# Later requests for masks and residuals, earlier rows for the next group, and a reordered last gate in a graph layer kernel

## The chip, the cores and the metric

The kernel runs on one core of one Trainium2 chip. The metric is the device time of one execution in microseconds (us). Of several executions the median is given; one further execution was profiled, and every number on instructions, waits and transfers comes from that one.

## The reference

The input is a batch of 32 graphs of 512 nodes with 256 features, and a 512 x 512 mask `adj` for each. All numbers are 32-bit floats. The layer is, for each graph:

```
h      = relu(layernorm(x))
c1     = relu(bn1(conv1d_1tap(h)))                 # 256 -> 256 channels
x_conv = relu(bn2(conv1d_17taps(c1)) + h)          # along the 512 nodes
s      = h @ w_se.T + b_se                         # 3 numbers a node
A      = exp(-|s_n - s_m|^2) * adj                 # 512 x 512
x_nmp  = A @ relu(h @ w_msg.T + b_msg)
gi     = concat(x_conv, x_nmp) @ w_ih.T + b_ih     # 512 -> 768
gh     = h @ w_hh.T + b_hh                         # 256 -> 768
r, z   = sigmoid of the first two thirds of gi + gh
new    = tanh(gi_n + r * gh_n)
out    = x + (1 - z) * new + z * h
```

So there are three large blocks of matrix work: the 17-tap convolution, the masked product of the graph, and the gates r, z and new.

## The kernel before

**Layout.** A graph's features stand with channels on partitions (`hT`, two halves of 128 channels by 512 nodes). The 17-tap convolution is computed with a fast algorithm: the nodes of all graphs are cut into units of 18, the units are collected in seven groups (`STARTS`), and each group takes 25 products of transformed inputs (`x2`, `xd`) with transformed weights (`w`). In the first group the weights are made on the chip and stored to DRAM (`wd`); from the second group on they are read back through a ring of three buffers. In the second group VectorE also forms a third of each weight by an addition (`third_weight`).

**Streams.** The program is not written out by hand. Five Python generators, called streams, give out work: `rows` (one-tap convolution of the graphs of a group, `conv1`, which fills the group's input `h1`), `begins` (normalise and transpose a graph), `graphs` (messages, exponentials, mask, masked product), `conv` (the 25 products of each group) and `gates`. A loop at the end of the kernel function keeps a modelled time `now` for TensorE and modelled free times for VectorE and ScalarE (`dve.free`, `act.free`). A stream yields the modelled time at which it may go on, or a condition. Of the streams that may go on, the loop takes the one whose clock is furthest behind its share. `fill()` then lets VectorE run ahead of `now` by up to 1.5 us of modelled work. What comes out is one fixed order of instructions for each engine[...]. `later(t, f)` puts an action off to modelled time t, and `settle()` runs everything that was put off, at once.

**Queues.** Nearly all loads are issued by SyncE (SP) in one order: masks (`Graphs.ask`, a ring of four), residuals (`load_res`, a ring of two), weights, rows (`load_row`, in the ring of two `hT` buffers that the transposed graphs also use), and the inputs of the gates. A load into a buffer that is still in use waits at the head of the SP queue. Stores are issued by GpSimd (POOL).

**Lines that matter here.** `masked` (L887) multiplies one quarter of the exponentials by the mask and asks for the next mask at once. `update` (L1129), run with each z gate, asks for the other residual: `load_res(b + o, 1 - o)`. `all_rows` (L1259) starts a group's rows when `at_product >= 25 * g - 1`, that is, when the last product of the group before is taken up. In `gates`, after the z products, the stream runs `reset_hidden` (VectorE: (r + 1) times the hidden product) and yields `dve.free + 0.1` before the products of the new gate. For the very last half gate (the last graph, o = 1) the hidden product is cut in two parts (384 and 128 nodes), which are multiplied after the z gate; `mix_ahead` (L1080) is four VectorE instructions that prepare the output before the tanh.

**A product of groups 2 to 7.** Eight matmul records with `x2` (called x products below) go to one bank of `ps_c`; ScalarE copies the bank to its neighbour; sixteen records with `xd` (xd products) then add to both banks; ScalarE takes the result away. The exponentials of a graph (L877) use the same `ps_c` buffer for one of their four matmuls. Each float32 matmul of the program is two records in the profile.

## Time and profile before

| what | value |
|---|---|
| median of 3 executions | 2123.65 us (2122.25 to 2126.0) |
| the profiled execution, its own time | 2125.44 us |
| its span | 2123.3 us |
| TensorE busy | 2062.8 us, 97% of the span |
| VectorE busy | 1375.5 us, 65% |
| ScalarE busy | 815.2 us, 38% |
| GpSimd busy | 337.7 us, 16% |
| granted TensorE clock, mean | 0.989 |
| transfers | 383.07 MB, 180 GB/s on average |

PE is TensorE's matmuls, PEld its weight loads, DVE VectorE, ACT ScalarE, POOL GpSimd, SP SyncE. L126 and L135 are helper lines through which nearly all instructions are recorded, so groups are told apart by the tiles that they write and read. A row of the waits reads: engine, what it was about to do, what ended its idle time, then us in total, number of waits and the longest. A row of the timeline reads: start, duration, engine, line, operation, tiles, shapes, count, and in brackets the idle time before it with its releaser. A row of a table by stage gives the stretch, its length, the busy time of PE, PEld, DVE, ACT and POOL (with counts), the granted clock, the busy share of the DMA engines and GB/s.

### The profile page before, as it was taken

What the parts mean: (1) busy time and instruction counts of PE and PEld (TensorE: products, weight loads), DVE (VectorE), ACT (ScalarE), POOL (GpSimd) and SP (SyncE); (2) the same over time, 40 slices, a digit from 0 to 9 for tenths busy, and PEclk for the clock granted to TensorE, in tenths of its full rate; (3) what the DMA queues carried; (4) which work ended last, traced back from release to release, by engine and by line L of the source; (5) the groups of instructions that cost most, each with busy time, mean ns of one, the idle gap of its engine ahead of it and who ended that gap; (6) DMA issues with size and microseconds to landing.
All of it is one profiled execution on the core that took longest, in us unless ns stands there. A gap on an engine that the chain in (4) does not pass through costs nothing.

```text
span 2123.3 us, 25913 instructions
## 1 busy us (share of the span) xinstructions
PE 2062.8 (97%) x8768; PEld 1265.0 (60%) x8768; DVE 1375.5 (65%) x2448; ACT 815.2 (38%) x1431; POOL 337.7 (16%) x582
## 2 busy tenths in 40 slices
PE   9999799999999989999999999999999999999998
PEld 6888366655666646666556665456665566654443
DVE  6888477884768737786576765576875757653223
ACT  5544533334532335422454233544324532234121
POOL 2101121111201102111121111121111210112111
PEclk9999999999999999999999999999999999999999
DMA  7455887776776676676767777677676756525332
GB/s 280 165 184 180 273 231 197 196 180 206 210 198 173 209 171 183 187 214 174 201 190 204 189 186 202 181 181 216 191 187 180 190 163 175 150 64 139 86 92 40
DMA packets 546436, 383.07 MB, mean 180 GB/s; under 512 B 456576, under 2 KB 473472, under 8 KB 545664
## 3 DMA queue, kind: packets, MB, share of 16 engines
q1 hardware_dynamic: 512992, 282.17, 50.5%
q0 software_dynamic: 28624, 86.01, 12.9%
q10 hardware_dynamic: 4688, 13.24, 1.6%
q8 instruction: 70, 1.15, 0.2%
q14 instruction: 62, 0.51, 0.1%
HBM read 281.95 MB, written 99.35 MB: 180 GB/s over the span
## 4 chain that ended last, share of the span: by engine, by line
PE 93%; ACT 2%; DMA 2%; DVE 1%; issue 1%; SPq 0%; POOL 0%; ACTq 0%; DVEq 0%
PE ps_acc L135 46%; PE ps_c L135 24%; PE ps_g L135 20%; DMA hT<-hd 2%; PE ps_g L140 2%; PE ps_c L877 1%; ACT at L126 0%; PE ps_acc L145 0%; DMA w<-wd 0%; ACT z L126 0%; PE ps_acc L877 0%; DMA vec<-in_vecs_dram 0%; ACT n L126 0%; ACT part L126 0%; PE ps_g L877 0%
## 5 line engine op out<-in xcount | busy, mean ns | idle before, releaser
L135 PE MATMUL ps_acc<-xconv,wih 128*128 128x512 f32 (+1 forms) x772 | 363.9, 594 | 3.5 <-DVE ps_acc L126 2.1
L135 PE MATMUL ps_acc<-xnb,wih 128*128 128x512 f32 (+1 forms) x772 | 362.3, 593 | 0.0
L135 PE MATMUL ps_acc<-hTb,whh 128*128 128x512 f32 (+1 forms) x772 | 357.3, 592 | 0.0
L135 PEld LDWEIGHTS ps_c<-xd,w 128*128 128x128 f32 x2400 | 300.2, 191 | 70.4 <-issue 56.3
L135 PE MATMUL ps_c<-xd,w 128*128 128x135 f32 (+1 forms) x2400 | 304.8, 280 | 4.8 <-ACT ps_c L126 4.8
L135 PEld LDWEIGHTS ps_c<-x,w 128*128 128x128 f32 x2000 | 253.5, 192 | 88.7 <-issue 54.7
L135 PE MATMUL ps_c<-x,w 128*128 128x135 f32 (+2 forms) x2000 | 262.4, 280 | 17.5 <-ACT z L126 6.3
L1093 POOL DMA_DIRECT2D out_dram<-res x252 | 164.0, 657 | 640.0 <-DVE res L126 580.4
L135 PEld LDWEIGHTS ps_acc<-xconv,wih 128*128 128x128 f32 x772 | 140.9, 191 | 147.5 <-issue 141.3
L135 PE MATMUL ps_g<-at,msg 128*128 128x512 f32 x512 | 227.4, 592 | 0.5 <-DVE at L126 0.5
L135 PEld LDWEIGHTS ps_acc<-hTb,whh 128*128 128x128 f32 x772 | 140.6, 190 | 144.8 <-issue 142.5
L135 PEld LDWEIGHTS ps_acc<-xnb,wih 128*128 128x128 f32 x772 | 141.0, 191 | 140.4 <-issue 138.4
L126 DVE TENSOR_TENSOR o_sb<-hTb,r 128x512 f32<-128x512 f32 x63 | 43.5, 690 | 211.3 <-ACT r L126 211.3
L135 PEld LDWEIGHTS ps_g<-at,msg 128*128 128x128 f32 x512 | 95.2, 190 | 110.5 <-issue 106.4
L126 DVE TENSOR_TENSOR msg<-ps_g,bmsg 128x256 f32<-128x256 f32 x128 | 53.8, 421 | 148.3 <-PE ps_g L135 148.2
L126 DVE SCALAR_TENSOR_TENSOR x<-x,x 128x544 f32<-128x544 f32 (+5 forms) x161 | 137.9, 856 | 3.3
L126 ACT ACTIVATE ps_c<-ps_c 128x270 f32<-128x270 f32 (+1 forms) x150 | 57.6, 384 | 206.1 <-PE ps_c L135 206.1
L135 PE MATMUL ps_g<-hT,w 128*128 128x512 f32 (+4 forms) x288 | 121.3, 570 | 14.7 <-DMA hT<-hd 14.7
L126 DVE TENSOR_TENSOR xd<-x 128x544 f32<-128x544 f32 (+1 forms) x150 | 107.4, 719 | 37.4 <-PE ps_c L135 37.2
L126 DVE TENSOR_TENSOR x<-x 128x272 f32<-128x272 f32 (+5 forms) x280 | 127.0, 499 | 0.3
L135 PE MATMUL ps_g<-wmsg,hTg 128*128 128x259 f32 x496 | 121.3, 381 | 0.0
L126 ACT ACTIVATE h<-ps_g,bn_shift,bn_scale 128x252 f32<-128x252 f32 (+4 forms) x208 | 85.8, 487 | 84.8 <-PE ps_g L135 84.7
(124 smaller groups left out, 2278.3 us busy)
## 6 DMA issues: line engine op xcount, KB each, us to landing
w<-wd SPq DMA_DIRECT2D x125, 768.0 KB, 5.2
m_sb<-in_adj_dram SPq DMA_DIRECT2D x384, 64.0 KB, 3.4
hd<-hT POOLq DMA_DIRECT2D x32, 512.0 KB, 6.0
hT<-hd SPq DMA_DIRECT2D x32, 512.0 KB, 4.6
hTb<-hd SPq DMA_DIRECT2D x32, 512.0 KB, 5.1
xnb<-nd SPq DMA_DIRECT2D x64, 256.0 KB, 3.3
xconv<-cd SPq DMA_DIRECT2D x32, 512.0 KB, 5.4
res<-in_x_dram SPq DMA_DIRECT2D x256, 64.0 KB, 3.8
```

The lines of the kernel that those rows point to most:

```text
L126: getattr(self.engine, name)(*tiles, **more)
L135: nc.tensor.matmul(ps, lhsT, rhs, **more)
L140: nc.tensor.transpose(ps, a, ident)
L877: nc.tensor.matmul(pss[c], gr.left[k, :], gr.right[k, :], start=True, stop=True, tile_position=(32 * c, 0),)
L1093: queue.dma_start(OB[b][:, s.start // 32 : s.stop // 32, o * P + 32 * g : o * P + 32 * g + 32], y[at, s].rearrange("i (k j) -> i k j", j=32),)
```

## The change

It has five parts.

1. In `masked`, from the ninth graph on, the next mask is asked for 1.5 us of modelled time after the mask's transpose, instead of right after the multiplication; a mask that was not asked for by then is asked for when it is needed.
2. A residual's buffer is asked for 5 us of modelled time after the store that empties it, instead of with the z gate; `mix_last` and `mix_ahead` ask for it if that has not happened.
3. The products of the new gate wait for `hidden_at`, the modelled end of `reset_hidden` plus 0.3 us, instead of `dve.free + 0.1`.
4. A group's rows may start when product `25 * g - 4` is taken up instead of `25 * g - 1`.
5. For the last half gate, the hidden product in two parts is computed before the z gate, and the `settle()` and the wait ahead of the remaining products go.

```diff
     def masked(b, at, c):
+        if (b, c) not in gr.masks:
+            gr.ask(NT * b + c + 1 - gr.asked)
...
         dve.transpose(gr.right, gr.masks.pop((b, c)))
+        later(dve.free + 1.5, lambda: gr.ask(1))
         dve.tensor_tensor(at[:, c, :], gr.right, at[:, c, :], op=ALU.mult)
-        gr.ask(1)
...
         def mix_last(r, z, o, s):
+            load_res(b, o)
             y = XR[b, o]
...
         def mix_ahead(z, o):
+            load_res(b, o)
             y = XR[b, o]
...
             if s.stop == N:
                 del XR[b, o]
+                later(now + 5.0, lambda: load_res(b + 1, o))
...
-                if b == o == 0:
+                if b == 0:
                     load_res(b, o)
...
+            hidden_at = 0.0
             def reset_hidden():
+                nonlocal hidden_at
                 while halves:
...
+                    hidden_at = dve.free + 0.3
...
             def update():
                 nonlocal z
-                load_res(b + o, 1 - o)
...
             if ps_h is not None:
                 reset_later(ps_h)
+            else:
+                parts = []
+                for s in (slice(0, N - P), slice(N - P, N)):
+                    ps = acc.tile([P, N], F32, name="ps_acc")
+                    parts.append((ps, s))
+                    for i in range(ND):
+                        matmul(
+                            ps[:, s], whh[:, i, cols(o, 2)], hT[:, i, s],
+                            start=(i == 0), stop=(i == ND - 1), skip_group_check=True,
+                        )
+                    hidden_half(ps, s)
+                    reset_later(ps, s)
+                    yield now
             ps_z = acc.tile([P, N], F32, name="ps_acc")
...
                 reset_hidden()
-                yield dve.free + 0.1
+                yield hidden_at
...
             later(act.free + 0.2, lambda: mix_ahead(z, o))
-            parts = []
-            for s in (slice(0, N - P), slice(N - P, N)):
...
-                yield now
-            settle()
-            yield dve.free + 0.1
             for ps, s in parts:
...
-                    freed >= g - 1 and begun > b and not turning and at_product >= 25 * g - 1
+                    freed >= g - 1 and begun > b and not turning and at_product >= 25 * g - 4
```

More of the change, by code (lines that the diff above doesn't have):

```diff
@@ L1178, in gates @@
             later(act.free + 0.2, lambda: mix_ahead(z, o))
-            parts = []
-            for s in (slice(0, N - P), slice(N - P, N)):
-                ps = acc.tile([P, N], F32, name="ps_acc")
-                parts.append((ps, s))
-                for i in range(ND):
-                    matmul(
-                        ps[:, s], whh[:, i, cols(o, 2)], hT[:, i, s],
-                        start=(i == 0), stop=(i == ND - 1), skip_group_check=True,
-                    )
-                hidden_half(ps, s)
-                reset_later(ps, s)
-                yield now
-            settle()
-            yield dve.free + 0.1
             for ps, s in parts:
```

## The prediction

> **What bounds the kernel now.** I read the page first: busy times and the chain that ended last.

> ```profile
> PE 2062.8 (97%) x8768; PEld 1265.0 (60%) x8768; DVE 1375.5 (65%) x2448; ACT 815.2 (38%) x1431; POOL 337.7 (16%) x582
> ...
> PE 93%; ACT 2%; DMA 2%; DVE 1%; issue 1%; SPq 0%; POOL 0%; ACTq 0%; DVEq 0%
> ```

> TensorE sets the end: 93% of the chain is matmuls, and no other engine is above 65%. So a change that leaves the matmuls alone can gain only what TensorE loses between them. Next, what TensorE waited for:

> ```profile
> PE ps_g L135 <- DMA hT<-hd: 14.7, 4, 7.9
> PE ps_c L135 <- ACT z L126: 6.6, 4, 4.8
> PE ps_c L135 <- ACT at L126: 6.0, 9, 0.7
> PE ps_c L135 <- ACT n L126: 5.1, 6, 1.3
> PE ps_c L135 <- ACT ps_c L126: 4.8, 9, 0.5
> ...
> PE ps_acc L135 <- DVE ps_acc L126: 2.1, 1, 2.1
> ```

> The first row is the loads of a new group's rows. The others are products placed right behind what they depend on, and the tail. Ends of matmuls are modelled, so I also took the distance of consecutive matmul starts less what such a matmul takes in a dense stretch (429 ns for 512 columns, some 113 ns for 135): TensorE loses about 78 us in all that way. The table by stage and the timeline show the largest place, where the second group begins:

> ```profile
> 210.42 0.49 SPq L830 DMA_DIRECT2D whh<-in_w_hh_dram  x1
> 210.96 0.94 SPq L831 DMA_DIRECT2D wih<-in_w_ih_dram  x1
> ...
> 215.22 0.40 SPq L210 DMA_DIRECT2D hT<-hd  x1
> ```

> ```profile
> 221.00:230.00 9.00, 1.05 (x3) 0.29 (x2) 2.55 (x3) 1.66 (x5) 1.08 (x2) 0.71 1.01 396
> 230.00:235.00 5.00, 5.00 (x7) 1.90 (x7) 0.69 (x1) 1.27 (x3) 0.54 (x1) 0.50 1.13 299
> 235.00:240.00 5.00, 5.00 (x15) 2.52 (x14) 0.00 (x0) 1.75 (x4) 0.00 (x0) 0.99 0.73 180
> ```

> The row load of 215.22 stands behind 2.25 MB of gate weights and takes 14.4 us in the chain; TensorE idles until 229.7 and then runs at half clock (0.50) for 5 us more. The same happens at 764 to 778. Last, an uncovered product and the tail:

> ```profile
> 1234.34 1.08 PE L135 MATMUL ps_c<-x,w 128*128 128x135 f32 x8
> 1235.95 1.30 PE L135 MATMUL ps_c<-xd,w 128*128 128x135 f32 x9 [0.53 <-ACT ps_c L126]
> ```

> ```profile
> 2111.80 0.69 DVE L126 SCALAR_TENSOR_TENSOR res<-part,res 128x512 f32<-128x512 f32 x1
> 2112.41 0.76 DVE L126 SCALAR_TENSOR_TENSOR ps_acc<-r,ps_acc 128x384 f32<-128x384 f32 x2
> 2113.02 1.56 PE L135 MATMUL ps_acc<-xconv,wih 128*128 128x384 f32 x4 [2.10 <-DVE ps_acc L126]
> ```

> Eight x records issue in 0.91 us; the xd product starts 1.61 us after their start: 0.70 us lost to ScalarE's copy. In the tail VectorE does `mix_ahead` first and TensorE's last products wait behind it.

> [...] SP stands 193.2 us in 51 waits for stores before residual loads, and 163.2 us in 51 before masks. [...]

> **The change part by part.** No work goes: the built programs have the same instructions on every engine, but for 4 warm-up transposes fewer (0.11 us each, put in where TensorE has nothing else). What moves is order, and I compared the two built orders.

> *Rows earlier.* Each batch's 512 KB load (issued in 0.3 to 0.4 us, landing in 4.6 at the median), its `conv1` matmuls, their six ACT evacuations (1.27 us for three) and the POOL memsets (about 0.5 us a boundary, 203.8 to 204.2) move some three products up. On SP all five loads of the second group now stand ahead of the 2.25 MB of gate weights. For every load I took the matmul work standing between what releases it and its first use: before, the shortest was 4.3 us, the load that stalled 5.9 us at 772; now the shortest is 8.9 us, the next 10.5, against 4.6 us of landing. So the 14.7 us go, hidden by products and gates; without that cover each load would cost up to 4.6 us. Half clock lasted about 5.3 us from 229.7 and 5.2 us from 772.8 (0.52), at half speed a loss of 2.65 and 2.5: 5.2 us go too. Moved ahead of stores on POOL, 0.5 us meets an engine 84% idle. Gate weights come later, but first use is some 17 us of matmuls off, against 12.7 us for the longer to land.

> *`hidden_at`.* `dve.free` is up to 1.5 us ahead of `now`, so the gates often could not go on and the scheduler put an xd product directly behind its x product. In the built order such pairs fall from 9 to 0, and an x product directly behind the last xd product from 7 to 0. From starts: 9 x 0.69 = 6.2 us, and 6 x 0.93 = 5.6 us (the seventh is the 4.8 us wait at 474, a late weight, left as it is). An exponential directly behind its transposes falls from 2 to 1: 1.4 us. Products directly behind the exponentials rise from 9 to 11: 2 x 0.82 = 1.6 us lost. If `hidden_at` is too early, the new gate waits for VectorE; the instruction takes 0.70 us and 0.3 is added, and matmuls whose feeder is under 1 us of matmul work back fall from 30 to 9. From nothing to 2 us; I take nothing.

> *Masks and residuals.* They cost TensorE nothing now: masks are used 29 us of matmuls or more after they are asked for, residuals 15 or more, and they land in 3.4 and 3.8. After: 24 and 18. Their price is what queues behind them on SP: weights, rows, gate inputs. Later masks leave SP freer. But residuals come nearer to their stores (median 3.5 us of matmuls between, before 6.4), since `settle()` often runs the delayed request at once. Before, the waits were 193.2/51 = 3.8 us each; I bound the change by -2 to +3 us for a request, hidden behind the covers above. What is late next is weights of group 2: loads with under 11 us of matmul work ahead of VectorE's addition rise from 10 to 13 (shortest 4.5; before 3.4). One of the ten cost 4.96 us and 1.7 us of half clock. I add 1.

> *Last gate.* VectorE's two parts now stand ahead of `mix_ahead`, which runs beside 3.5 us of matmuls: 2.1 us.

> Sum: -14.7 -5.2 -6.2 -5.6 -1.4 +1.6 -2.1 +1 = -32.6 us. The span becomes 2123.3 - 32.6 = 2090.7. The profiled execution took 2125.4, 1.8 over the median; against the median it is 2123.65 - 32.6 = 2091 us.

> **The rivals.** *Stalls come back elsewhere* (0.20). A scheduler's estimates miss anew in a new order. For it: VectorE stood 46.1 us in 20 waits for transposed input, with 14.7 in one, and the weights above. Two more stalls of 4.96 + 1.7 and a row load late by 4 give +17: about 2108. Against it: the fewer thin covers.

> *Residuals block SP, and it is slower* (0.08). The place is the row and weight loads queued behind a residual waiting for its store. Rows have about 13 us of cover less 4.6, so blocking decides from 8 us on; the longest now is 15.4. Above that each late load costs its delay and the clock, some 6.6 us as at 474. It takes five or more such (33/6.6), and with seven it is 2137. Only four residual requests fall among group 2's thin weight loads, which speaks against it.

> *Nothing comes of it* (0.04): row loads stall wherever they stand and the idle time moves: 2120 to 2127. Against it: the load at 215 was late because of what was ahead of it.

> *More comes of it* (0.06): the weight's stall (6.7) and the remaining half-clock stretches (about 8.5) vanish too: 2091 - 15 = 2076.

> **How the numbers follow.** The likeliest case (0.62) is 2091, its own range 2081 to 2101. 2078 to 2113 holds it, most of the second case and part of the last. About 0.2%, 4 us, is what a measurement of this kernel can tell from no change. Faster: 0.62 + 0.20 + 0.06 = 0.88; same 0.04; slower 0.08.

> **What would show it.** TensorE's wait for `hT<-hd` near zero and clock 1.00 around 215 to 240 and 765 to 780; nine waits for ACT `ps_c` gone; no DVE `ps_acc` wait in the tail; waits for `at` about 7 us. Wrong it would be with new TensorE waits behind late weights near 235 to 470 us, or with SP waiting for stores well over 193 us and rows late behind it.

## The result, and the profile after

The changed kernel takes 2117.15 us (median of 11, 2109.4 to 2122.01) against 2125.33 us for the kernel before (median of 11, 2122.25 to 2130.3): a ratio of 0.996, with a 95% interval of 0.9945 to 0.9974. It is faster by 8 us. 33 were forecast, and 2117 lies outside the range given. The profiled execution of the changed kernel took 2120.44 us, 3 us above the median, with a span of 2118.6.

The page, first its busy times, then the chain that ended last:

```profile
PE 2063.9 (97%) x8764; PEld 1263.2 (60%) x8764; DVE 1369.5 (65%) x2448; ACT 815.5 (38%) x1431; POOL 340.4 (16%) x582
...
PE 80%; issue 10%; DVE 3%; DMA 3%; ACT 2%; POOL 1%; SPq 1%; POOLq 0%; DVEq 0%; ACTq 0%
```

TensorE still sets the end. Four records fewer, the warm-up transposes, are all that is gone from it. Its waits in the changed kernel:

```profile
PE ps_g L135 <- DMA hT<-hd: 11.8, 6, 6.9
PE ps_acc L135 <- ACT xconv L126: 6.8, 1, 6.8
PE ps_c L135 <- ACT at L126: 6.7, 10, 0.7
PE ps_c L135 <- ACT ps_c L126: 3.5, 3, 1.9
PE ps_c L135 <- DVE x L126: 3.5, 1, 3.5
PE ps_g L140 <- DVE augl L126: 3.3, 1, 3.3
```

The wait for row loads, which was to go, is 11.8 us where it was 14.7. Nine waits for ScalarE's copy in `ps_c` have become three, but the three take 3.5 us where the nine took 4.8. The wait for `xconv`, an input of the gates, is 6.8 us where it was 1.4. Two waits for VectorE are new: 3.5 us for `x`, the transformed input of the convolution, and 3.3 us for `augl`, an input of the exponentials. The waits of the SP queue in the changed kernel show what has grown:

```profile
SPq L919 <- DMA out_dram<-res: 471.5, 104, 27.4
...
SPq L338 <- DVE right L126: 39.5, 16, 9.5
```

Before, SP stood 193.2 us in 51 waits for a store ahead of a residual load; now 471.5 us in 104. One request is four loads into a buffer that four stores empty, so SP can wait more than once for one request. Grouped by request, 23 of the 64 requests waited before, 8.4 us each, and 14 of them over 8 us; in the changed kernel 53 wait, 8.9 us each, and 27 of them over 8 us. The waits ahead of masks went the other way, from 163.2 to 39.5 us. The tail did as forecast. TensorE and VectorE in the timeline of the changed kernel:

```profile
2106.70 1.88 PE L135 MATMUL ps_acc<-xnb,wih 128*128 128x512 f32 x4
2108.42 1.45 PE L135 MATMUL ps_acc<-xconv,wih 128*128 128x384 f32 x4
```

```profile
2103.67 0.76 DVE L126 SCALAR_TENSOR_TENSOR ps_acc<-r,ps_acc 128x384 f32<-128x384 f32 x2 [2.75 <-ACT ps_acc L126]
2109.34 0.69 DVE L126 SCALAR_TENSOR_TENSOR part<-z,hTb 128x512 f32<-128x512 f32 x1 [4.91 <-ACT z L126]
```

VectorE's part (2103.67) now precedes `mix_ahead` (2109.34), and the last products follow without a gap: the 2.1 us are gone.

**How a residual request stalls TensorE.** The largest stall after is 6.9 us near 1380. From the timeline of the changed kernel, SP, then POOL, then TensorE:

```profile
1344.35 7.22 SPq L338 DMA_DIRECT2D m_sb<-in_adj_dram  x11
1356.66 1.97 SPq L919 DMA_DIRECT2D res<-in_x_dram  x4
...
1361.05 4.72 SPq L919 DMA_DIRECT2D x_sb<-xd  x8
...
1375.84 0.32 SPq L210 DMA_DIRECT2D hT<-hd  x1
```

```profile
1352.14 2.62 POOL L1097 DMA_DIRECT2D out_dram<-res  x4 [5.06 <-DVE right L126]
...
1370.21 0.54 POOL L954 DMA_DIRECT2D hd<-hT  x1 [6.13 <-DVE hT L126]
```

```profile
1382.05 2.62 PE L135 MATMUL ps_g<-hT,w 128*128 128x171 f32 x8 [6.88 <-DMA hT<-hd]
```

Read from the top: SP is done with its masks at 1351.6 and then stands for 4.9 us, because the next entry is a residual load whose buffer is being stored; POOL issues that store only at 1352.1. So the transposed input of the next graph (`x_sb<-xd`), behind the residual and four mask loads, leaves at 1361.1. VectorE's transposes wait for it, the store `hd<-hT` waits for VectorE (6.13 us), the row load waits for that store, since both use the two `hT` buffers, and TensorE waits 6.88 us for the row. The clock granted for the next 5 us is 0.50.

The other stall of that length, 6.8 us for `xconv` until 1712.1, looks different on SP:

```profile
1690.20 9.33 SPq L338 DMA_DIRECT2D m_sb<-in_adj_dram  x16
1701.12 2.11 SPq L919 DMA_DIRECT2D res<-in_x_dram  x4
1703.34 0.44 SPq L230 DMA_DIRECT2D xconv<-cd  x1
```

Issuing sixteen mask loads takes SP 9.33 us; in the same stretch it waits only 1.4 us for stores. The load of `xconv` stands mainly behind masks here. What the mask part has to do with it shows below.

### The profile page after: what moved, and what is told of

It reads as the page before. It is cut to its first block, busy times and chain, and to the rows that moved or that the text cites. A ratio compares the mean times of both kernels' runs of the same rounds, so it can differ in the third digit from the quotient of the medians.

```text
span 2118.6 us, 25907 instructions
## 1 busy us (share of the span) xinstructions
PE 2063.9 (97%) x8764; PEld 1263.2 (60%) x8764; DVE 1369.5 (65%) x2448; ACT 815.5 (38%) x1431; POOL 340.4 (16%) x582
## 4 chain that ended last, share of the span: by engine, by line
PE 80%; issue 10%; DVE 3%; DMA 3%; ACT 2%; POOL 1%; SPq 1%; POOLq 0%; DVEq 0%; ACTq 0%
PE ps_acc L135 40%; PE ps_c L135 21%; PE ps_g L135 17%; PE ps_g L140 1%; PE ps_c L877 1%; POOL out_dram L1097 1%; DMA hT<-hd 1%; DMA w<-wd 0%; DVE x L126 0%; PE ps_acc L145 0%; ACT at L126 0%; SPq L338 0%; PE ps_g L877 0%; DMA x_sb<-in_x_dram 0%; DMA xconv<-cd 0%
## 5 line engine op out<-in xcount | busy, mean ns | idle before, releaser
L135 PE MATMUL ps_acc<-xconv,wih 128*128 128x512 f32 (+1 forms) x772 | 365.2, 596 | 6.8 <-ACT xconv L126 6.8
L135 PE MATMUL ps_acc<-xnb,wih 128*128 128x512 f32 (+1 forms) x772 | 362.3, 594 | 0.0
L135 PE MATMUL ps_acc<-hTb,whh 128*128 128x512 f32 (+1 forms) x772 | 355.6, 590 | 0.0
L135 PEld LDWEIGHTS ps_c<-xd,w 128*128 128x128 f32 x2400 | 299.3, 190 | 73.2 <-issue 61.6
L135 PEld LDWEIGHTS ps_c<-x,w 128*128 128x128 f32 x2000 | 252.6, 191 | 90.7 <-issue 63.6
L135 PE MATMUL ps_c<-xd,w 128*128 128x135 f32 (+1 forms) x2400 | 302.2, 279 | 3.6 <-ACT ps_c L126 3.5
L135 PE MATMUL ps_c<-x,w 128*128 128x135 f32 (+2 forms) x2000 | 259.9, 278 | 13.8 <-ACT at L126 6.7
L135 PEld LDWEIGHTS ps_acc<-xconv,wih 128*128 128x128 f32 x772 | 141.6, 191 | 150.9 <-issue 140.9
L135 PE MATMUL ps_g<-at,msg 128*128 128x512 f32 x512 | 227.8, 596 | 0.6 <-DVE at L126 0.5
L135 PEld LDWEIGHTS ps_acc<-xnb,wih 128*128 128x128 f32 x772 | 141.2, 191 | 139.4 <-issue 136.8
L135 PEld LDWEIGHTS ps_acc<-hTb,whh 128*128 128x128 f32 x772 | 140.5, 190 | 139.6 <-issue 137.3
L126 DVE TENSOR_TENSOR msg<-ps_g,bmsg 128x256 f32<-128x256 f32 x128 | 53.8, 421 | 194.5 <-PE ps_g L135 194.2
L135 PEld LDWEIGHTS ps_g<-at,msg 128*128 128x128 f32 x512 | 95.6, 191 | 110.3 <-issue 105.1
L126 DVE TENSOR_TENSOR o_sb<-hTb,r 128x512 f32<-128x512 f32 x63 | 43.5, 690 | 172.2 <-ACT r L126 172.1
L126 DVE SCALAR_TENSOR_TENSOR x<-x,x 128x544 f32<-128x544 f32 (+5 forms) x161 | 137.7, 855 | 2.8
L135 PE MATMUL ps_g<-hT,w 128*128 128x512 f32 (+4 forms) x288 | 123.2, 577 | 11.9 <-DMA hT<-hd 11.8
L126 ACT ACTIVATE ps_c<-ps_c 128x270 f32<-128x270 f32 (+1 forms) x150 | 58.0, 387 | 196.2 <-PE ps_c L135 196.1
L126 DVE TENSOR_TENSOR xd<-x 128x544 f32<-128x544 f32 (+1 forms) x150 | 107.0, 718 | 40.1 <-PE ps_c L135 39.9
L126 DVE TENSOR_TENSOR x<-x 128x272 f32<-128x272 f32 (+5 forms) x280 | 126.9, 498 | 0.2
L135 PE MATMUL ps_g<-wmsg,hTg 128*128 128x259 f32 x496 | 123.7, 382 | 0.0
L126 ACT ACTIVATE h<-ps_g,bn_shift,bn_scale 128x252 f32<-128x252 f32 (+4 forms) x208 | 85.8, 486 | 75.5 <-PE ps_g L135 75.4
```

The lines of the kernel that those rows point to most:

```text
L126: getattr(self.engine, name)(*tiles, **more)
L135: nc.tensor.matmul(ps, lhsT, rhs, **more)
```

## The experiments

Theory A: the parts do what was forecast, and the residual requests take most of it back through the SP queue. Theory B: a new order brings about as many gaps as it removes, whatever the residuals do. Each experiment was timed against runs of the kernel before in its own comparison (medians 2122.7 to 2123.7 us). Where medians of different comparisons are subtracted below, the ratios give up to 3 us less.

**Three residual buffers, nothing else.** The order of instructions on every engine is that of the changed kernel; only the wait goes.

```diff
-            XR[b, o] = late.tile([P, N], F32, name="res", bufs=2)
+            XR[b, o] = late.tile([P, N], F32, name="res", bufs=3)
```

> The changed kernel with three residual buffers instead of two, and every engine's order unchanged, so that a residual request no longer waits for the store just before it. Theory A (the residual requests, standing behind their stores, hold the SP queue and make row, gate-input and weight loads late; that is where the expected gain went): SP's wait for stores before residual loads falls from 471 us to under 50, TensorE's waits for hT<-hd and for ACT xconv fall from 11.8 + 6.8 us to under 5 together, and the time falls by 15 to 25 us, to 2093 to 2102. Theory B (a new order always brings some 70 us of new gaps, whatever the residuals do): the SP wait falls but other waits take its place, 2112 to 2120.

Measured: 2092.72 us (2090.93 to 2094.98), ratio 0.9857 (0.9842 to 0.9871). This is the fastest kernel measured but for one that equals it, below. Its waits, SP's and TensorE's:

```profile
SPq L919 <- DMA out_dram<-res: 37.9, 21, 6.1
```

```profile
PE ps_acc L135 <- ACT xconv L126: 4.6, 1, 4.6
...
PE ps_g L135 <- DMA hT<-hd: 2.1, 2, 1.4
```

SP's wait for stores is 38 us, row loads cost 2.1, and 24 us come back. SP's waits of all kinds hardly change in total: 1405 us before, 1420 in the changed kernel, 1372 here. It stands about as long, but for other things. Since the order is that of the changed kernel, theory B does not hold. `xconv` keeps most of its wait: theory A expected under 5 us for the two together, and they are 6.7. At the place shown above, the timeline of this kernel reads:

```profile
1338.00 1.95 SPq L919 DMA_DIRECT2D res<-in_x_dram  x4
...
1342.21 4.67 SPq L919 DMA_DIRECT2D x_sb<-xd  x8
...
1357.29 0.32 SPq L210 DMA_DIRECT2D hT<-hd  x1
```

```profile
1363.49 1.40 PE L135 MATMUL ps_g<-hT,w 128*128 128x171 f32 x8 [1.38 <-DMA hT<-hd]
```

The residual load follows the masks at once (their last ended at 1337.8), and the stall of 6.88 us is 1.38 us.

**The kernel before with three residual buffers**, the same edit there.

> The kernel before with three residual buffers, order unchanged. Theory A: before, the requests came with the z gate and waited 193 us for stores in all; the large stalls (hT behind the gate weights, uncovered products) have another cause and stay, so 0 to 6 us are gained: 2119 to 2125. Theory B: no change, 2122 to 2128. If instead it gains 15 us or more, the residual wait was already a main loss before the change.

Measured: 2121.91 us, ratio 0.9994 (0.9985 to 1.0002). SP's wait for stores falls from 193 to 43 us, and by the interval at most 3 us are gained. That doesn't tell theory A from theory B, but it excludes that the residual wait was a main loss before the change. In the old order the same kind of wait was hidden.

**The change without its residual part.** The request stands in `update` again.

```diff
-                later(now + 5.0, lambda: load_res(b + 1, o))
...
+                load_res(b + o, 1 - o)
```

> The changed kernel with its residual part undone: residuals are asked for with the z gate as before, the rest stays. Theory A: SP's waits for stores fall back to about 190 us, and the time goes to 2092 to 2105. Theory B: the scheduler's new order has its own stalls, 2110 to 2122.

Measured: 2099.86 us, ratio 0.9889 (0.9873 to 0.9904); SP waits 230.5 us for stores, more than the 190 expected. Theory A's range for the time holds.

**The residual part alone**, on the kernel before.

> The kernel before with the residual part of the change alone. Theory A: SP's waits for stores rise to 400 us or more and the kernel is slower than before, 2130 to 2150. Theory B: within 6 us of the kernel before, 2119 to 2131.

Measured: 2136.32 us (2129.46 to 2138.26), ratio 1.0058 (1.0043 to 1.0073): slower. SP in this kernel:

```profile
SPq L917 <- DMA out_dram<-res: 551.2, 111, 18.2
```

So the part costs about 13 us in the old surroundings and 17 in the new ones (2117.15 to 2099.86, from different comparisons).

**Later requests, still two buffers.** Is it the nearness of a request to its store? Here it goes on a list that `fill()` alone runs, not `settle()`, due 12 us after the store.

```diff
-                later(now + 5.0, lambda: load_res(b + 1, o))
+                ASKS.append((now + 12.0, lambda: load_res(b + 1, o)))
```

> The changed kernel, two residual buffers, but a residual request is held on a list of its own that settle() does not run, and for 12 us of modelled time after the store instead of 5. TensorE's order is unchanged; between a store and the request that waits for it stand 12.0 us of matmul work at the median instead of 3.5. If it is the nearness to the store that holds up SP, its waits for stores fall from 471 to under 200 us and the time goes to 2093 to 2102. If residual requests cost by their number or place in another way, it stays at 2110 to 2120.

Measured: 2097.33 us, ratio 0.9877 (0.9857 to 0.9897). SP's line:

```profile
SPq L919 <- DMA out_dram<-res: 67.3, 34, 9.8
```

So the requests cost by standing near their stores, and moving them away helps without a third buffer. Both halves of the edit seem to be needed, by built orders that were not run: the list alone (still 5 us) and the 12 us alone (still in `later`) leave the median at 3.5 us of matmul work between store and request. There 5 us of modelled time are too short, and a longer delay is cut short by `settle()`.

**One part taken out, with three buffers.** These ask what the other parts are worth; the edits undo the lines of the diff.

> Three residual buffers and the change without its rows part (a group's rows wait again for product 25g-1). The built order has 2 xd products directly behind their x product (after: 0). If the rows part is worth what the prediction put on it (14.7 us of waits for row loads, 5.2 us of half clock), the wait for hT<-hd comes back at the second group's begin and at one or two later ones, 10 to 15 us, and the time is 2107 to 2114 against 2092.7. If instead the earlier new gates alone (hidden_at) already gave TensorE enough other work at the boundaries, it stays at 2093 to 2098.

Measured: 2118.15 us, 25 more than with the part and above both ranges. TensorE's waits:

```profile
PE ps_g L135 <- DMA hT<-hd: 16.5, 3, 7.7
PE ps_acc L135 <- ACT xconv L126: 10.0, 3, 4.7
```

The row waits are back in full, and `xconv`, from the same queue, is later too.

> Three residual buffers and the change with the new gates waiting for dve.free + 0.1 again. The built order has 5 xd products directly behind x products, 4 x products directly behind xd products, 2 exponentials directly behind transposes and two more products directly behind exponentials. By the prices of the prediction: 5 x 0.69 + 4 x 0.93 + 1.4 + 2 x 0.82 = 10 us more than 2092.7, that is 2100 to 2105. If adjacency isn't what costs, 2090 to 2096.

Measured: 2112.82 us, 20 more, twice what the prices gave. The uncovered products are there (5.4 us for `ps_c` below), but so are other waits for ScalarE's results. Five x products stand behind the last xd product with only one or two gate steps of four records between, and start some 1.45 us late each, waiting for `z` or `n`; only pairs with nothing between had been counted. By the working of the table below, about 5 of the 20 us are half clock.

```profile
PE ps_c L135 <- ACT z L126: 8.6, 7, 1.6
PE ps_c L135 <- ACT ps_c L126: 5.4, 7, 1.9
```

> Three residual buffers and the change without its mask part (masks asked for right after the multiplication). TensorE's order is the same as in the changed kernel. SP's wait for VectorE before masks rises from 68 us to 150 or more. If the mask part matters for what stands behind the masks, 2095 to 2100; if its waits are hidden, 2091 to 2095.

Measured: 2092.13 us (2091.13 to 2099.81), the same as with the mask part. SP's wait before masks rises from 68 to 186.1 us:

```profile
SPq L338 <- DVE right L126: 186.1, 43, 13.9
```

```profile
PE ps_g L135 <- DMA hT<-hd: 8.6, 3, 6.6
```

The equal time hides an exchange of two stalls. Near 1340 SP waits 13.9 us at once for the buffer of a mask; the chain that was followed near 1380 in the changed kernel is late again, and TensorE waits 6.6 us for a row where it was 1.4. In return the masks ahead of `xconv` leave earlier, in two bursts of eight loads, and TensorE waits 0.2 us for `xconv` instead of 4.6. So the waits before masks are not hidden: in these two traces the mask part takes one stall away and brings another of about the same length.

> Three residual buffers and the change without its residual part, so that residuals are asked for with the z gate. TensorE's order is the same as in the changed kernel. If only the waits of SP for stores matter, and not where the requests stand, it equals the changed kernel with three buffers: 2090 to 2095. If earlier requests crowd out row loads, 2096 to 2101.

Measured: 2098.2 us (2092.73 to 2103.01), ratio 0.988 (0.9858 to 0.9902), against 0.9857 (0.9842 to 0.9871) for the changed kernel with three buffers. The intervals overlap, and this stays open: the later requests may be worth 5 us once they don't wait. The kernel differs from the one without the residual part, above, by the third buffer alone. SP waits 36.4 us for stores here and 230.5 there, and the times, 2098.2 and 2099.86 us, can't be told apart. So a total of SP waits does not give the cost; it matters which requests wait, and what stands behind them.

**Rows still earlier**, at product 25g-6, with three buffers.

> Three residual buffers and the change, with a group's rows starting at product 25g-6 instead of 25g-4. If rows are early enough already, nothing is to be gained at the boundaries, and two xd products directly behind x products come back (1.4 us): 2090 to 2097. If row loads still cost, up to 3 us less: 2088 to 2092.

Measured: 2112.74 us (2106.95 to 2114.52): a clear miss, 20 us slower than 25g-4. SP and TensorE in this kernel:

```profile
SPq L210 <- DMA hd<-hT: 48.4, 8, 12.7
```

```profile
PE ps_g L135 <- DMA hT<-hd: 13.9, 6, 5.0
PE ps_g L135 <- DVE aug L126: 6.5, 3, 3.8
```

The row loads now wait more for stores out of the `hT` ring that they share (48.4 us, with 25g-4 23.3), and the messages of the graphs for VectorE.

**One part alone, on the kernel before.**

> The kernel before with the rows part of the change alone. By the prediction's prices: 14.7 + 5.2 us for row loads, 4 x 0.69 + 3 x 0.93 us for uncovered products that go in this order, 4 x 0.82 us for products behind exponentials that come: 22 us less, 2098 to 2106. If the row loads stall wherever they stand, 2115 to 2124.

Measured: 2114.46 us, ratio 0.9954 (0.9938 to 0.9969): 8 us, not 22. The waits for row loads are gone, and with them 14 us. But there are still products with too little other work between them and what they depend on (thin covers, below), and waits for VectorE have come that the price did not hold: 3.5 us for `x` and 3.1 for `augl`. Of the thin covers, the waits for `z` are those of the experiment with late gates, where 5 and 4 pairs stand uncovered as here.

```profile
PE ps_c L135 <- ACT at L126: 8.7, 13, 0.7
PE ps_c L135 <- ACT z L126: 8.6, 7, 1.7
PE ps_c L135 <- ACT ps_c L126: 5.2, 7, 1.7
```

> The kernel before with the hidden_at part alone. By the prediction's prices: 7 x 0.69 + 6 x 0.93 + 2 x 1.4 - 2 x 0.82 = 11.5 us less, 2108 to 2116. If new stalls take their place, 2117 to 2125.

Measured: 2125.32 us, ratio 1.0015 (1.0007 to 1.0023): nothing gained, slower by 0.15%. Most thin covers went, and row loads and `xconv` took all of it:

```profile
PE ps_g L135 <- DMA hT<-hd: 23.2, 6, 9.4
PE ps_acc L135 <- ACT xconv L126: 11.1, 3, 5.3
```

**All of it accounted for.** For each profiled execution, gaps are the distances of consecutive matmul starts less the dense spacing (as in the prediction, from 0.06 us on), and the clock's loss is what matmuls that started at half clock lost by it.

| kernel | gaps us | clock us | span us | span less both |
|---|---|---|---|---|
| before | 78.4 | 15.2 | 2123.3 | 2029.7 |
| changed | 70.0 | 17.6 | 2118.6 | 2031.0 |
| changed, 3 residual buffers | 51.2 | 7.2 | 2089.1 | 2030.7 |
| changed, requests after 12 us | 54.2 | 10.0 | 2094.9 | 2030.7 |
| changed without residual part | 54.8 | 13.4 | 2099.0 | 2030.8 |
| before, residual part alone | 84.0 | 13.8 | 2127.5 | 2029.7 |
| before, rows part alone | 72.4 | 11.9 | 2113.3 | 2029.0 |
| before, gates part alone | 77.5 | 15.3 | 2123.6 | 2030.8 |

The last column is constant within 2 us: matmul work that no edit touches. All that these kernels differ by is how long TensorE stood, and how long it then ran at half clock. The table divides the time; it does not say what caused a gap.

## Why the prediction was wrong

**The bound was right.** TensorE sets the end, and the gain can come only from its gaps and its clock; the table shows it.

**The failing step is the pricing of the residual requests at nothing.** The prediction saw that they come nearer to their stores (3.5 us of matmul work at the median instead of 6.4) and bounded the effect by "-2 to +3 us for a request, hidden behind the covers above". Both halves of that failed. The 3.8 us is the mean of 51 waits, not of requests; by request it was 8.4 us for the 23 that waited. Spread over all 64 requests, the wait went from 3.0 to 7.4 us, so by 4.4, above the bound of 3: hardly by longer waits, but by 53 requests waiting instead of 23. Those over 8 us, from which the prediction had blocking decide, were 14 before and 27 after. And the 278 us more that SP stood for stores were not hidden. The covers counted only the matmul work between a load's release and its use. They left out the queue in which the load stands and the chain behind it, which at 1380 runs through SP, VectorE, POOL and SP again.

The prediction had named the sign, SP waiting for stores well over 193 us and rows late behind it, and had the mechanism as a rival with 0.08, as one that ends slower than before. It came at a third to a half of that price (17 us by leaving the part out, 24 by the third buffer, where the rival had 46, from 2091 to 2137), and so the time ended between the two cases. The reason given for the nearness, `settle()`, seems to be half of it: by the built orders the 5 us were too short as well.

**Without that step most of the sum came, but its terms did not.** With requests at the z gate the time is 2098 to 2100 us, 23 to 26 less than its kernel before; with the later requests and the third buffer it is 2092.7, 30 less, where the sum had 32.6. In the traces, from before to three buffers, the gaps fall by 27.2 us, and the terms of the sum without the clock make 27.4. That they agree so closely is luck, for the terms do not: row loads 14.7 to 2.1 us (forecast: to 0); waits for the `ps_c` copy 4.8 to 1.7; waits of `ps_c` products for `z` and `n` 11.7 to 2.4, a gain of 9.3 where 5.6 was forecast; waits for `at` 6.0 to 6.7 (forecast: about 7); the tail 2.1 to 0; half clock 15.2 to 7.2, a gain of 8.0 where 5.2 was forecast; and three waits of over 3 us each that the sum does not have (`xconv` 4.6, `x` 3.5, `augl` 3.2).

**Adding the parts was wrong.** Rows alone were to give 22 us and gave 8; the gates part alone was to give 11.5 and gave nothing. Leaving either out of the three-buffer kernel costs 25 or 20, so each is worth its price, and more, only beside the other. The gates part alone removed most of the thin covers, and more TensorE time went to row loads that were still asked for late (23.2 us); rows alone removed those, left thin covers and brought waits for VectorE. Why the gates part makes late rows worse stays open.

**Smaller points.** The mask part is worth nothing measurable beside three buffers, as forecast, and its wait on SP fell as forecast; but that is two stalls exchanged, and was not foreseen. Late weights of the second group, priced at +1, did not become a main loss, but they are there: the wait for `augl` near 330 stands behind one (VectorE, which makes `augl`, sits idle for 7.84 us until the weight lands and starts again at 327.2), while the stall of 4.96 us at 469, which the sum left in place, is gone from the changed kernel. That row loads moved ahead of the gate weights lose their stall was right: TensorE's wait of 8 us at the second group's begin is gone from the changed kernel. In its place stands the wait of 3.5 us for VectorE's `x`, a term that the prediction did not have; it is in every kernel here whose rows start at 25g-4 and in no other. So the clock from 215 to 240 is 0.95, up from 0.80 and not 1.00 as forecast; from 765 to 780 it is 1.00.

## What to carry to other kernels

A load asked for right behind the store that frees its buffer did not cost its own wait here: it cost the lateness of the loads behind it in the queue, and of what those loads feed (near 1380, 6.88 us of TensorE behind a wait of 4.9 us on SP, and 1.38 us with the third buffer). A total of waits does not tell this, and neither does their mean: group the waits by request, and see what stands behind each. Count the cover from where the load can leave the queue, through each engine that it passes, not from the release of its buffer alone. Before delaying a request, look whether one more buffer takes the wait away (here SP's 471.5 us for stores became 37.9); and when parts of a change remove different waits of one engine, measure them together as well as alone, since the wait that is left can grow (here the row loads, 14.7 us before and 23.2 with the gates part alone).

## What had not been expected of the hardware

The changed kernel scatters over 12.6 us (2109.4 to 2122.0) with one fixed order, and the scatter goes with the clock: the fastest run has a mean granted clock of 0.993, the slowest 0.987, and 0.006 of 2115 us is 12.7 us. A stall of about the same length is followed by half clock for quite different times. Here are stages after the two 7 us stalls of the changed kernel, two for the first and one for the other; the clock is the third number from the end:

```profile
1382.00:1387.00 5.00, 4.95 (x11) 3.44 (x12) 1.52 (x2) 1.49 (x4) 0.40 (x1) 0.50 0.31 74
1387.00:1392.00 5.00, 5.00 (x21) 2.15 (x20) 3.58 (x9) 2.86 (x6) 0.61 (x1) 0.92 0.91 255
...
1712.00:1717.00 5.00, 4.91 (x14) 2.70 (x15) 2.78 (x11) 1.95 (x5) 0.56 (x1) 0.65 0.05 18
```
